# A Nyström attention block with an expert network: the iterated inverse on fewer products, in one stream, with a planner that looks at the end

## The chip, the cores and the metric

The kernel runs on one core of one Trainium2 chip. The metric is device time in microseconds of one execution. A core has five engines that run at the same time and are ordered among each other by semaphores alone: TensorE (PE in the profile; its weight loads are listed as PEld), VectorE (DVE), ScalarE (ACT), GpSimd (POOL) and SyncE (SP, used here only to start DMAs). Each engine works through its own list of instructions in the order in which the program gives them.

## What is computed

The input is 16 sequences of 1024 rows of 256 values, float32 throughout. Cut to what matters:

```
x = x + layernorm(attention(layernorm(x)))
x = x + layernorm(expert_ffn(layernorm(x)))

attention, per sequence and for 16 heads of 16 columns:
    Q, K, V = x @ w_qkv;  Q = Q / 4
    Q_l, K_l = means of 16 successive rows of Q, K        # 64 rows each
    kernel1 = softmax(Q @ K_l.T)                           # 1024 x 64
    kernel2 = softmax(Q_l @ K_l.T)                         # 64 x 64
    kernel3 = softmax(Q_l @ K.T)                           # 64 x 1024
    SV = (kernel1 @ iterative_inv(kernel2)) @ (kernel3 @ V)
    return SV @ w_proj

iterative_inv(K):                                          # 6 iterations
    V = K.T / max(column sums of K)
    for _ in range(6):
        KV = K @ V
        V = (0.25 * V) @ (13 I - KV @ (15 I - KV @ (7 I - KV)))
    return V

expert_ffn: a base product, and for each of 8 experts a hidden layer and a
    reconstruction of the input; the sequence takes the adapter of the expert
    with the smallest reconstruction error
```

The change is about `iterative_inv`, about the order in which the pieces are given to the engines, and about what is prepared before the first batch.

## The kernel before

A batch is one sequence. Its work is cut into stages, each written as a Python generator that yields at the start of every small stretch:

- `stage_a`: turns the normalized rows (`turned_rows`, tile pt_a), makes Q, K and V (pq, pv), the landmark means (`lm`, `bd`), the weights of kernel3 and their product with V (`u`). Its last part normalizes the next batch's input (`norm_a`, tile xa).
- `stage_p`: kernel2 and its inverse V, then w_bd = V times u.
- `stage_c`: kernel1, its product with w_bd, the projection with wproj_sb (po), the normalization and the residual (`added`, tile x1).
- `stage_d1` and `stage_d2`: the norm (`norm`, tile xn_d), the experts' hidden layers (ph) and reconstructions (pr, with the squares of df on ScalarE), the choice of the expert, the gather of its adapter, and the output (pf, y_d).

**The order** of everything on PE, ACT, DVE and POOL is written out before the program is built, by a planner in the same file (`planned`, from line 1192). Each yield carries a name, the names that it follows, and planned times on each engine: `mm(us, tiling, count)` for TensorE and `ew(engine, us, behind, mark)` for the others; a mark "aside" says that nothing that follows waits for that part, "free" that it frees a bank of PSUM. `streams()` makes five lists: stage_a of all batches; stage_p of the even ones; stage_p of the odd ones; stage_c; stage_d1 and stage_d2. At each point the planner tries the next stretch of every stream, runs its model on for AHEAD = 50 us by each of a few rules, and takes the stretch that has lost the least TensorE time by then. `progress` ranks what is ready: a stream of RANK r is meant to be r batches behind stage_a.

Two waits between stages matter. "bd" of batch b in stage_a follows "kp" of batch b - 1 in stage_p, and the products with w_bd in stage_c follow "end" of stage_p. A batch's inverse before the change has 31 stretches: six up to the first V ("kp", "k2", "k2n", "k2t", "rrow", "v0"), four in each of the six iterations ("kv", "sq", "t3", "v"), and "end".

**The inverse** keeps the 16 heads' 64 x 64 matrices as one tile of 128 x 8 x 64: eight on partitions 0 to 63, eight on 64 to 127. `product` (line 552) multiplies all 16 pairs in the 64x64 tiling of TensorE, four independent quarters. Both operands of a matmul lie on the same half of the partitions; which half the result goes to is free. A head is numbered by four bits r, s, t, p2, and `(half, slot)` says which bit chooses the partition half and which bits choose the place. The operand given as lhsT enters transposed, so the kernel keeps V in two forms (`vi` and its transpose `vt`), and K transposed (`k2t`). KV is made twice in an iteration, once with each of two bits as the half (tiles yx and yy, both with 7/3 of the identity taken off), because the third product needs it where the square lies:

```
pkv -> yx = KV - 7/3 I  (halves by x)     yy = KV - 7/3 I  (halves by y)
psq = yx.T yx           sq = psq - 4/3 I
pb  = sq.T yy           t3 = 92/27 I - pb
pvi = vt.T t3  -> vi = 0.25 pvi           pvi = t3.T vt  -> vt = 0.25 pvi
```

Tiles of the inverse come in two sets, `tag{b % 2}`, one for the even batches' stream and one for the odd.

**Before the first batch** the program starts DMAs on ScalarE's queue for all weights, the last of them bd1_rows and bd2_rows; makes the identity and several masks; takes the row means off wproj_sb and wbase_sb (`centre`, lines 148 to 156, on DVE); and transposes the two biases on TensorE (lines 191 to 197). The input of batch 0 is one DMA of 1 MB on SP's queue (`load`, line 116), followed by those of x1.

Of the kernel before, what the change touches and what calls it, by code (L numbers as in the profile page):

```python
# [19 lines left out]
AHEAD, GAP = 50.0, 1.0  # L20
# [25 lines left out]
def kernel(  # L46
# [69 lines left out]
    def load(b, tag, bufs):  # L116
        t = keep.tile([P, NT, D], F32, tag=tag, name=f"{tag}_{b}", bufs=bufs)
        nc.sync.dma_start(out=t, in_=x[b].rearrange("(t p) d -> p t d", p=P))
        live[b][tag] = t
# [13 lines left out]
    bd1_rows = work.tile([E // 2, P], F32, tag="e1", name="bd1_rows")  # L133
    nc.scalar.dma_start(out=bd1_rows, in_=bd1.rearrange("(i r) h -> i (r h)", r=2))
    bd2_rows = work.tile([E * NC, P], F32, tag="e1", name="bd2_rows")
# [18 lines left out]
    for c in range(NC):  # L154
        centre(wproj_sb[:, c, :])
        centre(wbase_sb[:, c, :])
# [34 lines left out]
    bias_ps = one_bank([P, 512], "bias_ps")  # L191
    nc.tensor.transpose(bias_ps[:, 0 : E // 2], bd1_rows, ident[: E // 2, : E // 2])
    nc.tensor.transpose(bias_ps[:, 64 : 64 + E * NC], bd2_rows, ident[: E * NC, : E * NC])
    bd1_sb = const.tile([P, E // 2], F32, name="bd1_sb")
    nc.scalar.copy(bd1_sb, bias_ps[:, 0 : E // 2])
    bd2_sb = const.tile([P, E, NC], F32, name="bd2_sb")
    nc.scalar.copy(bd2_sb.rearrange("p e k -> p (e k)"), bias_ps[:, 64 : 64 + E * NC])
# [36 lines left out]
    def go(name, follows, *parts):  # L234
        return name, follows, parts
# [292 lines left out]
    def stage_p(b):  # L528
# [9 lines left out]
        def mat(tag, name=None):  # L538
            return inv.tile([P, NP, M], F32, tag=f"{tag}{b % 2}", name=f"{name or tag}_{b}")
# [12 lines left out]
        def product(dst, a, c, to, rest):  # L552

            (x, x_at), (y, y_at) = a, c
            frm = x_at[0]
            for g0 in range(2):
                for g1 in range(2):
                    four = [h for h in heads if h[rest[0]] == g0 and h[rest[1]] == g1]
                    for h in sorted(four, key=lambda h: (h[frm] ^ h[to], h[frm])):
                        rows, i = place(*x_at, h)  # L560
                        rows_y, j = place(*y_at, h) if y_at else (rows, None)
                        assert rows_y == rows
                        nc.tensor.matmul(  # L563
                            dst[64 * h[to] : 64 * h[to] + 64, 4 * h[frm] + 2 * g0 + g1, :],
                            lhsT=x[rows, i, :],
                            rhs=y[rows, j, :] if y_at else y[rows, :],
# [13 lines left out]
        kp = inv.tile([P, NC, PC, M], F32, tag=f"yx{b % 2}", name=f"kp_{b}")  # L580
# [12 lines left out]
        mx = small.tile([P, NP], F32, tag=f"mx2{b % 2}", name=f"mx2_{b}", bufs=1)  # L593
# [5 lines left out]
        sm = small.tile([P, NP], F32, tag=f"sm2{b % 2}", name=f"sm2_{b}", bufs=1)  # L599
        nc.vector.tensor_reduce(sm, k2, X, ALU.add)  # L600
        rs = small.tile([P, NP], F32, tag=f"rs2{b % 2}", name=f"rs2_{b}", bufs=1)
# [8 lines left out]
        cs = small.tile([P, NP], F32, tag=f"cs{b % 2}", name=f"cs_{b}", bufs=1)  # L610
# [4 lines left out]
        cmx = small.tile([NP, 2], F32, tag=f"cmx{b % 2}", name=f"cmx_{b}", bufs=1)  # L615
        nc.vector.tensor_reduce(cmx, pcs, X, ALU.max)
        rmx = small.tile([NP, 2], F32, tag=f"rmx{b % 2}", name=f"rmx_{b}", bufs=1)
        nc.vector.reciprocal(rmx, cmx)
        rrow = inv.tile([NP, 2, M], F32, tag=f"yy{b % 2}", name=f"rrow_{b}")
# [4 lines left out]
        rd = small.tile([P, NP], F32, tag=f"rd{b % 2}", name=f"rd_{b}", bufs=1)  # L624
# [4 lines left out]
        x, y = "r", "s"  # L629
        for i in range(N_ITER):  # L630
# [3 lines left out]
            yield step(f"kv{i}", mm(2 * Q, "q64", 128), ew("dve", 0.6, 0), ew("dve", 0.6, 0, "free aside"))  # L634
            pkv = banks_of(f"pkv{i}")
            at_x = product(pkv[0], (k2t, kt_at), (vi, v_at), x, (y, "p2"))
            at_y = product(pkv[1], (k2t, kt_at), (vi, v_at), y, (x, "p2"))
            yx, yy = mat("yx"), mat("yy")
            nc.vector.tensor_tensor(yx, pkv[0], middle(eyes[0], NP), ALU.subtract)
            nc.vector.tensor_tensor(yy, pkv[1], middle(eyes[0], NP), ALU.subtract)  # L640
            parts = [mm(Q, "q64", 64), ew("dve", 0.6, -1, "free")]
            if i == 0:
                parts = [mm(Q, "q64", 64), *parts, ew("act", 0.5, 0, "free aside")]
            yield step(f"sq{i}", *parts)
            if i == 0:
                pvt = banks_of("pvt")
                vt_at = product(pvt[1], (vi, v_at), (eye, None), x, (y, "p2"))
            psq = banks_of(f"psq{i}")
            sq_at = product(psq[0], (yx, at_x), (yx, at_x), y, ("p2", "t"))
            sq = mat("vi", "sq")  # L650
            nc.vector.tensor_tensor(sq, psq[0], middle(eyes[1], NP), ALU.subtract)
            if i == 0:
                vt = mat("vt")
                nc.scalar.copy(vt, pvt[1])
            yield step(f"t3{i}", mm(Q, "q64", 64), ew("dve", 0.6, -1, "free"))
            pb = banks_of(f"pb{i}")
            t3_at = product(pb[0], (sq, sq_at), (yy, at_y), x, ("p2", "t"))
            t3 = mat("yx", "t3")
            nc.vector.tensor_tensor(t3, middle(eyes[2], NP), pb[0], ALU.subtract)  # L659
            more = i < N_ITER - 1  # L660
            yield step(
                f"v{i + 1}",
                mm(*((2 * Q, "q64", 128) if more else (Q, "q64", 64))),
                ew("act", 0.5, 0),
                ew("act", 0.5, 0, "free aside" if more else "free"),
            )
            pv = banks_of(f"pvi{i}")
            if more:
                v_at = product(pv[0], (vt, vt_at), (t3, t3_at), "t", (y, "p2"))
            vt_at = product(pv[1], (t3, t3_at), (vt, vt_at), y, ("t", "p2"))  # L670
            if more:
                vi = mat("vi")
                nc.scalar.mul(vi, pv[0], 0.25)  # L673
            vt = mat("vt")
            nc.scalar.mul(vt, pv[1], 0.25)
            x, y = y, x
# [7 lines left out]
        for r, half in halves():  # L684
            nc.scalar.copy(
                w_bds[b % 2][half, :, r, 0:HD], pw[half, r, 0 : NP * HD].rearrange("x (q d) -> x q d", d=HD)
            )


    def stage_c(b):  # L690
        w_bd = w_bds[b % 2]
        first = [("a", b, "bd"), *([("d", b - 2, "end")] if b >= 2 else [])]
        svt = [None] * NW
# [565 lines left out]
```

## Time and profile before

| | |
|---|---|
| median of three executions | 2420.9 us (2420.38 to 2425.7) |
| the profiled execution | 2422.45 us, span 2420.7 us |
| mean granted TensorE clock | 0.978 |
| DVE: yx, yy, sq, t3 of the inverse | 65.8, 65.3, 65.6, 65.2 us busy, 96 each |
| ACT: vt, vi of the inverse | 56.8 (96) and 47.5 us (80) busy |
| TensorE, products of the inverse by tile | pkv 115.1, psq 66.7, pb 65.5, pvi 65.3 and 57.0, pkt 12.1, pvt 10.9 us busy |

In the profile a group's line has the program line, the engine, the operation, the tile written and the tiles read, the shapes and the count; then busy time in us and the mean of one in ns; then how long the engine stood idle just before such instructions, with what ended it. A line of the timeline has the start, the length and the same names; what stands in brackets is the idle time before it and its releaser. A waits line has the total, the number of times and the longest. Matmuls overlap with their successors, so a group's busy time contains tails that run under the next group. A float32 matmul leaves two records. "issue" is time in which the engine waited for nothing that the profile shows.

### The profile page before, as it was taken

Reading aid. Unit: us, or ns where it says so; the run is one execution under the profiler, and the core shown is the slowest. Engines: PE = TensorE matmul, PEld = TensorE weight load, DVE = VectorE, ACT = ScalarE, POOL = GpSimd, SP = SyncE. Lnnn points to the kernel's source line nnn. Section 1 sums busy time; section 2 is a strip of 40 time slices with the busy share of each in tenths; the row PEclk is TensorE's granted clock in tenths of the full one; section 3 lists DMA queues with packets and bytes.
Section 4 is the critical chain, followed back from the end, with each engine's and each line's share of the span. In section 5 each row is a group of like instructions: output and inputs, shape, how many; then the busy total and the mean of one; then the engine's idle time right before and its main releaser. Section 6 shows DMA issues by size and latency. Waiting matters only on the chain.

```text
span 2420.7 us, 94984 instructions
## 1 busy us (share of the span) xinstructions
PE 2220.6 (92%) x43954; PEld 1458.7 (60%) x43954; DVE 1475.8 (61%) x2811; ACT 1241.5 (51%) x2467; POOL 272.2 (11%) x387
## 2 busy tenths in 40 slices
PE   5998999999999999999999999899999999898865
PEld 3666656575565756657565665656666575665442
DVE  4556576575747666576566657557575666655443
ACT  1333464564546556464745545455454555465545
POOL 1000011020110201011020200202011020111021
PEclk9999999999999999999999999999999999999888
DMA  3000001010010100101010010101001000010000
GB/s 109 19 21 3 20 5 55 2 34 25 5 54 3 57 2 5 54 6 54 2 57 2 14 45 3 55 3 32 27 5 55 2 21 21 5 38 26 15 21 20
DMA packets 56628, 60.94 MB, mean 25 GB/s; under 512 B 4964, under 2 KB 55208, under 8 KB 56232
## 3 DMA queue, kind: packets, MB, share of 16 engines
q1 hardware_dynamic: 50208, 50.35, 6.5%
q8 instruction: 345, 5.65, 0.9%
q0 software_dynamic: 2560, 2.14, 0.3%
q10 hardware_dynamic: 3464, 2.37, 0.3%
q14 instruction: 51, 0.42, 0.1%
HBM read 38.08 MB, written 16.78 MB: 23 GB/s over the span
## 4 chain that ended last, share of the span: by engine, by line
PE 43%; DVE 8%; ACT 7%; issue 2%; POOL 1%; DMA 0%; POOLq 0%; DVEq 0%; ACTq 0%
PE ph L899 5%; PE pq L339 5%; PE pr L932 4%; ACT df L943 3%; PE pf L1033 3%; PE po L829 2%; PE pv L360 2%; PE pvi L563 2%; PE pf L1034 2%; PE pkv L563 2%; PE psv L781 2%; PE psct L752 2%; DVE df L940 2%; DVE mx L417 1%; PE psct L760 1%
## 5 line engine op out<-in xcount | busy, mean ns | idle before, releaser
L943 ACT ACTIVATE df<-df,bd_sb 128x512 f32<-128x512 f32 x512 | 363.3, 711 | 165.4 <-DVE df L940 165.4
L940 DVE TENSOR_TENSOR df<-pr,xt_d 128x1024 f32<-128x1024 f32 x256 | 301.7, 1216 | 107.9 <-PE pr L932 68.5
L932 PE MATMUL pr<-ht,wd_sb 64*64 64x512 f32 x2048 | 251.0, 597 | 3.6 <-ACT ht L907 1.5
L899 PE MATMUL ph<-xt_d,wd_sb 128*128 128x512 f32 x512 | 236.3, 604 | 1.4 <-DVE maxima L722 0.8
L339 PE MATMUL pq<-xt_a,wqkv_sb 128*128 128x512 f32 x512 | 228.1, 600 | 0.0
L722 DVE TENSOR_REDUCE maxima<-psc 128x16 f32<-128x1024 f32 x128 | 150.3, 1217 | 76.9 <-PE psc L714 76.9
L770 ACT ACTIVATE e<-psct 128x1024 f32<-128x1024 f32 x128 | 124.0, 1020 | 115.3 <-PE psct L760 115.2
L417 DVE TENSOR_REDUCE mx<-psm 128x2 f32<-128x1024 f32 x128 | 149.7, 1216 | 33.5 <-PE psm L408 33.5
L339 PEld LDWEIGHTS pq<-xt_a,wqkv_sb 128*128 128x128 f32 x512 | 96.0, 192 | 114.3 <-issue 110.0
L899 PEld LDWEIGHTS ph<-xt_d,wd_sb 128*128 128x128 f32 x512 | 93.1, 191 | 117.1 <-issue 94.6
L453 ACT ACTIVATE e<-psc 128x1024 f32<-128x1024 f32 x128 | 122.8, 1025 | 73.2 <-PE psc L443 71.8
L1033 PE MATMUL pf<-wbase_sb,xt_d 128*128 128x256 f32 x512 | 136.6, 390 | 0.9 <-DVE t L659 0.9
L563 PEld LDWEIGHTS pkv<-vi,k2t 64*64 64x64 f32 x6144 | 104.1, 137 | 44.1 <-issue 18.2
L283 DVE SCALAR_TENSOR_TENSOR y_d<-y_d,rstd_d_y,x 128x256 f32<-128x256 f32 x128 | 53.3, 479 | 124.2 <-POOL rstd_d_y L250 124.1
L248 POOL TENSOR_SCALAR ve_c_y<-ss_c 128x4 f32<-128x4 f32 x32 | 6.2, 195 | 1086.6 <-ACT square_c L294 1086.6
L563 PE MATMUL pkv<-vi,k2t 64*64 64x64 f32 x6144 | 115.1, 223 | 8.0 <-ACT vi L673 3.3
L932 PEld LDWEIGHTS pr<-ht,wd_sb 64*64 64x64 f32 x2048 | 64.9, 133 | 95.5 <-issue 60.6
L829 PE MATMUL po<-wproj_sb,svt 128*128 128x256 f32 x512 | 120.1, 388 | 1.0 <-ACT svt L804 0.9
L781 PE MATMUL psv<-w_bd,e 128*32 128x34 f32 x8192 | 90.3, 198 | 33.0 <-issue 23.5
L781 PEld LDWEIGHTS psv<-w_bd,e 128*32 128x32 f32 x8192 | 80.0, 109 | 61.7 <-issue 35.7
L360 PE MATMUL pv<-wqkv_sb,xt_a 128*128 128x256 f32 x512 | 116.7, 381 | 0.0
L360 PEld LDWEIGHTS pv<-wqkv_sb,xt_a 128*128 128x128 f32 x512 | 95.9, 190 | 22.5 <-issue 7.8
(174 smaller groups left out, 4042.8 us busy)
## 6 DMA issues: line engine op xcount, KB each, us to landing
xa<-in_L_attn_x_dram SPq DMA_DIRECT2D x16, 1024.0 KB
x<-in_L_attn_x_dram SPq DMA_DIRECT2D x16, 1024.0 KB
out_dram<-y_d SPq DMA_DIRECT2D x32, 512.0 KB
wqkv_sb<-in_L_attn_w_qkv_dram ACTq DMA_DIRECT2D x1, 768.0 KB
wd_sb<-in_L_ffn_Wd_dram ACTq DMA_DIRECT2D x2, 256.0 KB
wd_sb<-in_L_ffn_Wd_dram ACTq DMA_DIRECT2D x1, 512.0 KB
wdn<-in_L_ffn_Wa_down_dram,row POOLq DMA_INDIRECT x32, 2.7
wproj_sb<-in_L_attn_w_proj_dram ACTq DMA_DIRECT2D x1, 256.0 KB
```

The source lines that it names most:

```text
L339: nc.tensor.matmul(pq[:, n, :], lhsT=wqkv_sb[:, k, f0 : f0 + P], rhs=xt[:, k, n * 512 : (n + 1) * 512], start=(k == 0), stop=(k == NC - 1),)
L360: nc.tensor.matmul(pv[:, j, :], lhsT=xt[:, k, (t0 + j) * P : (t0 + j + 1) * P], rhs=wqkv_sb[:, k, 2 * D : 3 * D], start=(k == 0), stop=(k ...
L417: nc.vector.tensor_reduce(mx3[:, n, q : q + 2], psc[g], X, ALU.max)
L563: nc.tensor.matmul(dst[64 * h[to] : 64 * h[to] + 64, 4 * h[frm] + 2 * g0 + g1, :], lhsT=x[rows, i, :], rhs=y[rows, j, :] if y_at else y[ro ...
L722: nc.vector.tensor_reduce(mx[:, t0 : t0 + 2, 64 * g : 64 * g + 64].rearrange("x t (p j) -> x p t j", p=2)[:, :, :, 0 : 2 * NC], psc[g].rea ...
L781: nc.tensor.matmul(psv[rows32(g), j // 2, col : col + 2 * (HD + 1)], lhsT=es[p // 2][:, p % 2, j * P + 32 * g : j * P + 32 * g + 32], rhs= ...
L829: nc.tensor.matmul(po[:, j, :], lhsT=svt[n][:, c, j * P : (j + 1) * P], rhs=wproj_sb[:, c, :], start=(c == 0), stop=(c == NC - 1),)
L899: nc.tensor.matmul(ph[:, n, :], lhsT=wd1_sb[:, k, 2 * i : 2 * i + 2, :].rearrange("p e h -> p (e h)"), rhs=xt[:, k, n * 512 : (n + 1) * 51 ...
L932: nc.tensor.matmul(pr[to, r, :], lhsT=wd2_sb[half, i, k * P + 64 * f : k * P + 64 * f + 64], rhs=ht[half, cols], start=True, stop=True,)
L940: nc.vector.tensor_tensor(df, pr, middle(xt[:, k, cols], 2), ALU.subtract)
L943: nc.scalar.activation(df[:, r, :], df[:, r, :], AF.Square, bias=bd2_sb[:, e, k : k + 1], accum_out=part[:, e, k * NW + n : k * NW + n + 1],)
L1033: nc.tensor.matmul(po[:, j, :], lhsT=xt[:, k, cols], rhs=wbase_sb[:, k, :], start=(k == 0), stop=False)
```

## The change

Five parts.

1. **The inverse.** Iterations go in pairs. In the first of a pair KV is made once, by its own product (`x_at`, half h); ScalarE copies it as it is to `xh`. The second form that the third product needs is no longer a product: `across` copies half of y to the other half of the partitions with two ScalarE copies (tile yc), and `product` takes its right operand from y or from that copy, by head. At the end of the first iteration, in place of the new V, the kernel makes the next KV from the old one: `px` = xh.T t3, which is 4 times K times the new V; y of the second iteration is 0.25 px less 7/3 of the identity, again with `across`. V is then made in its transposed form alone (`vt`). At the end of the second iteration both forms of V are made as before. A batch has 28 stretches and 28 products of 16 matmuls, where it had 31 and 37.
2. **One stream of inverses** over all batches instead of two, and one set of its tiles.
3. **Preparations as stretches:** the centring of wproj_sb becomes the first stretch of stage_c, that of wbase_sb with the transposes of the biases the first of stage_d1. bd1_rows and bd2_rows get their buffers from the tag "df".
4. **The load of batch 0's input** in two DMAs, four row blocks each.
5. **The planner:** it looks 70 us ahead instead of 50; progress is the stream's planned TensorE time done, scaled to the number of batches; when less than LAST = 250 us of planned TensorE work is left, each trial runs to the end of the program, counts the end of all engines, and has four more rules that favour the earlier stages.

```diff
-AHEAD, GAP = 50.0, 1.0
+AHEAD, LAST, GAP = 70.0, 250.0, 1.0
...
-        nc.sync.dma_start(out=t, in_=x[b].rearrange("(t p) d -> p t d", p=P))
+        rows = x[b].rearrange("(t p) d -> p t d", p=P)
+        for h in range(2 if b == 0 else 1):
+            part = slice(0, NT) if b else slice(4 * h, 4 * h + 4)
+            nc.sync.dma_start(out=t[:, part, :], in_=rows[:, part, :])
...
-    bd1_rows = work.tile([E // 2, P], F32, tag="e1", name="bd1_rows")
+    bd1_rows = work.tile([E // 2, P], F32, tag="df", name="bd1_rows", bufs=3)
...
-    for c in range(NC):
-        centre(wproj_sb[:, c, :])
-        centre(wbase_sb[:, c, :])
...
+    def prepare_c():
+        yield go(("c", 0, "weights"), [("a", 0, "qk", 0, 0)], ew("dve", 1.9, None))
+        for c in range(NC):
+            centre(wproj_sb[:, c, :])
+
+    def prepare_d():
+        yield go(
+            ("d", 0, "weights"), [("a", 0, "qk", 1, 0)], mm(0.2, "full", 4), ew("act", 0.3, -1, "free"), ew("dve", 1.9, None)
+        )
+        bias_ps = one_bank([P, 512], "bias_ps")
+        nc.tensor.transpose(bias_ps[:, 0 : E // 2], bd1_rows, ident[: E // 2, : E // 2])
+        nc.tensor.transpose(bias_ps[:, 64 : 64 + E * NC], bd2_rows, ident[: E * NC, : E * NC])
+        nc.scalar.copy(bd1_sb, bias_ps[:, 0 : E // 2])
+        nc.scalar.copy(bd2_sb.rearrange("p e k -> p (e k)"), bias_ps[:, 64 : 64 + E * NC])
+        for c in range(NC):
+            centre(wbase_sb[:, c, :])
...
         def mat(tag, name=None):
-            return inv.tile([P, NP, M], F32, tag=f"{tag}{b % 2}", name=f"{name or tag}_{b}")
+            return inv.tile([P, NP, M], F32, tag=tag, name=f"{name or tag}_{b}")
...
+                        yt = y[h[y_at[0]] ^ h[y[2]]] if isinstance(y, tuple) else y
...
+        f, h, g = "t", "r", "s"
+
+        def taken_y(px, scale):
+            y = mat("yx")
+            if scale == 1.0:
+                nc.vector.tensor_tensor(y, px, middle(eyes[0], NP), ALU.subtract)
+            else:
+                nc.vector.scalar_tensor_tensor(y, px, scale, middle(eyes[0], NP), ALU.mult, ALU.subtract)
+            return y
+
+        def across(y):
+            other = mat("yc", "across")
+            frm, to = (t.rearrange("x (f k p) m -> x f k (p m)", f=2, k=2) for t in (y, other))
+            for r, half in halves():
+                nc.scalar.copy(to[64 - 64 * r : 128 - 64 * r, :, r, :], frm[half, :, 1 - r, :])
+            return y, other
+
+        ACROSS = ew("act", 0.33, -1, "aside"), ew("act", 0.33, -1, "aside")
         for i in range(N_ITER):
...
+            if i % 2 == 0:
+                n = 2 if i == 0 else 1
...
+                px, pvt = banks_of(f"pkv{i}")
+                x_at = product(px, (k2t, kt_at), (vi, v_at), h, (g, "p2"))
+                if i == 0:
+                    vt_at = product(pvt, (vi, v_at), (eye, None), h, (g, "p2"))
+                y = taken_y(px, 1.0)
+                xh = mat("xx")
+                nc.scalar.copy(xh, px)
+                if i == 0:
+                    vt = mat("vt")
+                    nc.scalar.copy(vt, pvt)
+                y = across(y)
...
+            sq_at = product(psq[0], (y[0], x_at), (y[0], x_at), g, ("p2", f))
...
+            t3_at = product(pb[0], (sq, sq_at), ((*y, h), (g, (f, h, "p2"))), h, ("p2", f))
+            t3 = mat("vi", "t3")
...
+            if i % 2 == 0:
+                yield step(f"x{i + 1}", mm(2 * Q, "q64", 128), ew("dve", 0.65, 0), ew("act", 0.5, 0, "free aside"), *ACROSS)
+                px, pv = banks_of(f"px{i}")
+                x_at = product(px, (xh, x_at), (t3, t3_at), g, (f, "p2"))
+                vt_at = product(pv, (t3, t3_at), (vt, vt_at), g, (f, "p2"))
+                f, h, g = h, g, f
+                y = taken_y(px, 0.25)
+                vt = mat("vt")
+                nc.scalar.mul(vt, pv, 0.25)
+                y = across(y)
...
     def stage_c(b):
+        if b == 0:
+            yield from prepare_c()
...
     def stage_d1(b):
+        if b == 0:
+            yield from prepare_d()
+
...
-    RANKS = 0, 1, 1, 2, 3
+    RANKS = 0, 1, 2, 3
...
+        return [chain(stages) for stages in ([stage_a], [stage_p], [stage_c], [stage_d1, stage_d2])]
...
+        progress.append([rank + NB * at / sums[-1] for at in sums])
+
+    TOTAL = sum(sums[-1] for sums in before) - 1e-6
...
+            work = self.done()
+            return (self.clock["pe"] if work < TOTAL else max(self.clock.values())) - work + self.gaps
...
+    RULES = [(0.0, 0.1, 0.0), (1.0, 0.1, 0.0), (0.0, 0.3, 0.0), (1.0, 0.3, 0.0)]
+    LAST_RULES = [*RULES, (0.0, 0.1, 0.6), (0.0, 0.1, 1.5), (1.0, 0.1, 0.6), (1.0, 0.1, 1.5)]
...
+            return (wait if wait > 0.15 else 0.0), at - (stay if change == 0.0 else 0.0) + spread * RANKS[k]
...
+            ending = model.done() > TOTAL - LAST
+            limit = TOTAL * 2 if ending else model.clock["pe"] + AHEAD
...
-                    while trial.clock["pe"] <= model.clock["pe"] + AHEAD and (then := trial.next()):
+                    while trial.clock["pe"] <= limit and (then := trial.next()):
```

## The prediction

> **What bounds the kernel.** I read the busy shares first, then five windows of the span, then the groups of TensorE, the waits, and the timeline around the inverse's products.
>
> ```profile
> PE 2220.6 (92%) x43954; PEld 1458.7 (60%) x43954; DVE 1475.8 (61%) x2811; ACT 1241.5 (51%) x2467; POOL 272.2 (11%) x387
> ```
> ```profile
> 0.00:23.00 23.00, 0.76 (x4) 0.66 (x5) 9.17 (x46) 1.52 (x3) 6.63 (x23) 1.00 0.79 240
> 23.00:240.00 217.00, 197.60 (x4147) 136.38 (x4149) 126.06 (x239) 71.71 (x98) 9.19 (x15) 0.95 0.05 17
> 240.00:2180.00 1940.00, 1842.00 (x37517) 1215.68 (x37505) 1231.36 (x2321) 1043.62 (x2073) 220.41 (x303) 0.99 0.08 24
> 2180.00:2335.00 155.00, 131.56 (x2080) 81.89 (x2076) 75.17 (x140) 85.13 (x196) 23.11 (x30) 0.91 0.06 17
> 2335.00:2421.00 86.00, 48.71 (x234) 24.05 (x234) 34.01 (x69) 39.55 (x99) 12.85 (x17) 0.82 0.08 26
> ```
>
> The columns after the length are busy time of PE, PEld, DVE, ACT, POOL, then clock. In the middle 1940 us PE is idle for 98 (5%) while DVE and ACT have a third or more to spare: the middle is bound by TensorE's work. The other 102 idle us are the first 23 (22 idle), the filling (19), the draining (23) and the last batch alone (37).
>
> ```profile
> L563 PE MATMUL pkv<-vi,k2t 64*64 64x64 f32 x6144 | 115.1, 223 | 8.0 <-ACT vi L673 3.3 <-issue 2.4 <-ACT e L770 0.5
> L563 PE MATMUL pb<-yy,sq 64*64 64x64 f32 x3072 | 65.5, 223 | 10.5 <-DVE sq L651 9.9 <-DVE mx L417 0.4
> ```
> ```profile
> 2228.70 1.16 PE L563 MATMUL pkv<-vi,k2t 64*64 64x64 f32 x64
> 2230.77 0.69 PE L563 MATMUL psq<-yx 64*64 64x64 f32 x32 [0.91 <-DVE yx L639]
> 2232.36 0.69 PE L563 MATMUL pb<-yy,sq 64*64 64x64 f32 x32 [0.90 <-DVE sq L651]
> 2233.95 0.69 PE L563 MATMUL pvi<-vt,t 64*64 64x64 f32 x32 [0.89 <-DVE t L659]
> ```
>
> One product of an inverse is 32 records (16 matmuls, two each). The second fence shows an inverse with nothing beside it: 1.59 us from product to product.
>
> **The products removed.** Per batch, before: pkt 1, pvt 1, kv 12, sq 6, t3 6, v 11: 37. After: pkt 1, pvt 1, kv 3, sq 6, t3 6, x and its V 6, v 5: 28. So 9 x 16 = 144 fall away. Price: in the timeline of PE, 87 stretches of exactly one product between other tilings last 0.687 us on average from their start to the next group's start, 35 of two products 1.174. One more product therefore costs 0.487, and entering and leaving the tiling 0.20. 144 x 0.487 = **-70**. Bounds: by undisturbed stretches (1.09 less 0.62) 0.47, -68; by busy time (392.6 us of all seven product groups over 592 products) 0.663, -95, which counts pipeline tails that overlap the next group; so I stay near the first.
>
> **Visits to the tiling.** The 416 64x64 steps before (26 a batch) are joined into 340 visits, since two batches' inverses are in flight and meet. After there are 23 x 16 = 368, each waiting for the one before, so none join: 28 x 0.20 = **+6**; between 0 (joined with the 64x64 pr) and +15 (all 76 joins dear).
>
> **What ACT and DVE gain and lose.** DVE loses yy: 96 x 0.680 = 65 us. ACT loses 48 vi (0.593), gains 48 copies xh (0.58, as L654) and 192 half copies across partitions. The trace has none such; the nearest are the 128x256 copy ut at 0.376 and the 64x512 a_t, which changes partitions, at 0.682 for twice the columns. I take 0.40: 77 us, ACT at some 1318 of 2344, 56%. The scaled y (a scalar_tensor_tensor of 128x512) is priced like the others at 0.68. The halved buffers add no wait of their own, since the next inverse starts behind this one's end anyway. None of the rest is on TensorE as long as it is in time: t3 starts at the earliest two steps after kv, 3.18 us; y is ready at 0.69 + 0.2 + 0.68 = 1.57, the two copies at 2.6. Slack 0.6 if ACT is free; behind a pair of squares (2 x (0.711 + 0.187) = 1.8) they are 1.2 late. The plan doesn't make t3 wait for them, so it may place t3 too soon, and all of PE's later list stands behind it; on ACT the copies wait for y with exps and squares behind them. I take a tenth of 96 places late by 0.5: **+5**, between 0 and 96 x 0.4 = +38.
>
> **The start.**
>
> ```profile
> PE bias_ps L192 <- DMA bd_rows<-in_L_ffn_bd_dram: 19.9, 1, 19.9
> DVE mean L150 <- DMA wbase_sb<-in_L_ffn_W_base_dram: 4.4, 1, 4.4
> ```
>
> Two in-order queues stand behind late DMAs: PE until 19.9, DVE until 19.65, though batch 0's input had landed at 9.3. By 15.3 DVE had all but one of the statistics and had spent 0.85 on centring. Without the centring the last ends near 15.0, the norm begins there instead of at 22.14: **-7**. Bounds: -2.5 (only the centring behind the wait goes) to -9.5 (the first half of the split load also lands, say, a quarter sooner than 9.3, so that half the statistics lie before it). SP issues one DMA more, 0.43 us, ahead of the x1 loads, first read at 240: nothing. The centring (2 x 1.77 us of DVE), two transposes (0.5 of PE) and two tiny ACT copies come back later, in a filling where DVE is busy 126 of 217 us; uncovered they would cost 4.
>
> **The end.** Batch 15's second add_normalized ends at 2322.9, but DVE's list has batch 14's output first, held until 2334.3 by its rstd, so the statistics for 15 start at 2341. From there to the end 80 us are one batch's chain, which no order shortens. A plan that sees the end can have batch 14 done sooner: at most the 23 idle us before 2335 and some 3 of the next. Half: **-12**, between 0 and -26. The same longer look in the middle I put at 0: 5% idle is all there is.
>
> Sum: -70 + 6 + 5 - 7 - 12 = -78. The profiled execution took 2422.45 us (span 2420.7), 1.5 above the median 2420.9: 2344 by it, **2343** as a median.
>
> **Rivals.**
> *More than that* (0.13): all terms at their gains, -95 - 9.5 - 26 = -130: **2292**. For it: with one inverse in flight at a time latency falls from 147 us (batch 0, k2 at 50 to end at 197) or about 230 (later ones), so filling and draining shorten. Against: the middle was 95% full, busy counts tails. The Trainium skill (TensorE: Matmul & The Clock Gate, "Wait — 56ns, not 53.3ns?") says matmuls never start closer than about 25 ns; 32 a product would make 0.8 us and 144 of them -115, an estimate, a total near 2299. The rows disagree: 0.487 us for 32 is 15 ns, in a tiling of four independent tiles.
>
> *The copies are late* (0.10): +38 instead of +5, and nothing gained at the end: 2422 - 70 + 6 - 7 + 38 = **2389**. For it: ACT already waits 165.4 us for DVE with its list in order. Against: the slack of 0.6, and other work usually lies between sq and t3.
>
> *Slower, the single chain sets the end* (0.09): all sixteen inverses now stand in one row, 28 steps each (31 before). The first can't begin before 44, and after the last 185 us followed. A time of 2421 is reached when one inverse takes (2421 - 44 - 185)/16 = 137 us, 4.9 us a step: that is the point from which it decides, and batch 0's pace before was 147 us for 30 steps, also 4.9. At 5.1 it is 143 an inverse, **2517**. Against: undisturbed steps take 1.59, and the plan gives TensorE to the stream that lags. A stage also waits for it sooner: "bd" of batch b needs kp of b-1, now behind the end of b-2.
>
> *Slower, by the clock* (0.02): fewer streams leave holes, and the granted clock in the middle falls from 0.99 to 0.93, near the 0.95 of the filling, when few streams were ready: 0.06 x 1842 = 110 more, **2454**. Half clock comes in stretches of 3.4 us or multiples. The Trainium skill (same page, "HAM oscillation — how this bites in real kernels") warns of TensorE gaps over about 3.4 us; here the longest wait of an inverse's product is under 2.5, which is why I give it little.
>
> *It does nothing* (0.02): TensorE's freed time returns as waiting: 2422. Against it is the 95%.
>
> **How the numbers follow.** The forecast (0.64) covers 2320 to 2368. Faster by over 0.2% (5 us, about what three runs can tell from no change) takes it and the first two rivals: 0.87; same 0.02; slower 0.11. The range runs from the first rival's inner half to past the second: 2300 to 2400; left out are the slower cases, no change and the far ends.
>
> **What would show it.** Product records falling from 592 to 448 products (pkv to 2048 records, pvt now among them); TensorE busy near 2140; first pq near 19 instead of 26; middle idle still about 5%; no wait of pb for ACT over a few us; the last statistics less than 10 us after the last residual add. I am wrong if pb waits for the half copies, if the inverses run back to back with c waiting for w_bd, or if TensorE's idle in the middle grows past 170 us.

## The result, and the profile after

| | before | after |
|---|---|---|
| median | 2423.3 us (2420.38 to 2432.8, 4 runs) | 2361.23 us (2356.43 to 2365.14, 4 runs) |
| ratio | | 0.9738, 95% interval 0.9718 to 0.9757 |
| profiled execution | 2422.45 us, span 2420.7 | 2365.14 us, span 2363.4 |

62 us less, 2.6%. The forecast was 78 less. The kernel before took 2423 to 2426 us in some of the sets of runs and 2490 to 2501 in the others; so ratios to the kernel before of the same set are compared, and 0.1% of them is 2.4 us.

The busy shares of the kernel after:

```profile
PE 2164.1 (92%) x39346; PEld 1387.4 (59%) x39346; DVE 1424.0 (60%) x2715; ACT 1317.5 (56%) x2659; POOL 277.2 (12%) x387
```

TensorE does 56.5 us less and is idle as long as before, 199 us against 200. The same five windows of the kernel after; the middle ends 60 us earlier, the last two have nearly the lengths of before (columns as before):

```profile
0.00:23.00 23.00, 8.38 (x27) 5.67 (x28) 8.74 (x39) 4.06 (x4) 7.00 (x23) 1.00 0.95 282
23.00:240.00 217.00, 201.37 (x3917) 135.51 (x3916) 132.78 (x264) 90.28 (x134) 12.82 (x20) 0.98 0.06 17
240.00:2120.00 1880.00, 1769.55 (x33042) 1137.81 (x33041) 1171.20 (x2202) 1091.60 (x2212) 221.46 (x297) 0.99 0.08 24
2120.00:2275.00 155.00, 133.93 (x2128) 82.78 (x2127) 76.59 (x142) 91.77 (x212) 22.75 (x30) 0.91 0.06 17
2275.00:2363.00 88.00, 50.88 (x238) 25.59 (x236) 34.67 (x70) 39.76 (x99) 13.18 (x18) 0.79 0.08 26
```

The first window has 8 us more of TensorE's work, since the first pq starts 8 us sooner; its line of before, then of after:

```profile
26.07 14.46 PE L339 MATMUL pq<-xt_a,wqkv_sb 128*128 128x512 f32 x32
```
```profile
18.09 14.42 PE L351 MATMUL pq<-xt_a,wqkv_sb 128*128 128x512 f32 x32
```

In the middle it is idle for 110 of 1880 us (5.9%; before 98 of 1940). The end has gained nothing: 88 us with 37 idle, before 86 with 37.

TensorE's groups that answer to the two shown of before, and one that the change doesn't touch, whose line of before stands below it:

```profile
L577 PE MATMUL pkv<-vi,k2t 64*64 64x64 f32 x1536 | 35.2, 229 | 5.3 <-issue 2.6 <-ACT vi L723 1.8 <-DVE vi L641 0.6
L577 PE MATMUL pb<-yx,sq 64*64 64x64 f32 x1536 | 65.3, 223 | 16.3 <-DVE sq L692 8.8 <-ACT e L822 6.3 <-ACT vt L707 0.6
L577 PE MATMUL pb<-across,sq 64*64 64x64 f32 x1536 | 65.0, 223 | 2.1 <-ACT across L662 1.3 <-issue 0.9
L420 PE MATMUL psm<-kt,bd 32*128 32x512 f32 x512 | 93.7, 655 | 5.0 <-ACT e L822 1.2 <-DVE mx L429 0.9 <-DVE svn L844 0.9
```
```profile
L408 PE MATMUL psm<-kt,bd 32*128 32x512 f32 x512 | 86.0, 633 | 1.4 <-DVE k L596 0.5 <-ACT e L770 0.4 <-DVE df L940 0.4
```

The product of K with V is a quarter of what it was, and 592 products of the inverse are 448. The half copies (`across`) made TensorE wait twice, for 1.3 us. But psm, whose 512 matmuls are the same as before, has gone from 86.0 to 93.7 us.

ScalarE's groups that are new in the inverse:

```profile
L662 ACT COPY across<-yx 64x256 f32<-64x256 f32 x192 | 77.4, 403 | 3.4
L707 ACT ACTIVATE vt<-px 128x512 f32<-128x512 f32 x48 | 28.5, 593 | 62.4 <-DVE yx L655 62.1
L683 ACT COPY xx<-pkv 128x512 f32<-128x512 f32 x48 | 28.1, 585 | 67.2 <-DVE yx L653 67.1
```

The copies across cost what was forecast, 0.40 us. The other two rows hold something else: 129 us in which ScalarE stood idle until VectorE's y was done, which reads the same PSUM tile. In some 88 of them its own product had been done. The engines take turns on the tile, as one step near the end shows, in the timeline of TensorE, then VectorE, then ScalarE:

```profile
2153.89 0.69 PE L577 MATMUL pkv<-vi,k2t 64*64 64x64 f32 x32 [0.86 <-ACT vi L723]
...
2154.72 0.69 DVE L653 TENSOR_TENSOR yx<-pkv,eye 128x512 f32<-128x512 f32 x1 [3.08 <-PE pkv L577]
...
2155.45 0.59 ACT L683 COPY xx<-pkv 128x512 f32<-128x512 f32 x1 [1.12 <-DVE yx L653]
2156.05 0.82 ACT L662 COPY across<-yx 64x256 f32<-64x256 f32 x2
```

`xx` begins 0.04 us after y ends, though its product had been done since 2154.6. The copies across end 2.98 us after the product's start; the prediction had 2.6, since it let them follow y directly.

Another view of TensorE serves for what follows. **Occupancy** of a group: from the start of each of its stretches in TensorE's timeline to the start of the next group's, summed; it takes in waits and the changing of the tiling, and the groups together make the span. A **tiling change** is a place where two successive groups differ in tile shape.

| | before | after |
|---|---|---|
| occupancy of the inverse (kv, sq, t3, x, v, pkt, pw) | 395.0 us | 330.2 us |
| psm, pr, psc, put, pt_d together | 666.6 us | 700.3 us |
| psv and psct together | 253.2 us | 234.7 us |
| tiling changes | 1121 | 1185 |

### The profile page after: what moved, and what is told of

It is laid out like the page before. It is cut to its first block, busy times and chain, and to the rows that moved or that the text cites. A ratio compares the mean times of both kernels' runs of the same rounds, so it can differ in the third digit from the quotient of the medians.

```text
span 2363.4 us, 85848 instructions
## 1 busy us (share of the span) xinstructions
PE 2164.1 (92%) x39346; PEld 1387.4 (59%) x39346; DVE 1424.0 (60%) x2715; ACT 1317.5 (56%) x2659; POOL 277.2 (12%) x387
## 4 chain that ended last, share of the span: by engine, by line
PE 42%; DVE 8%; ACT 7%; issue 3%; POOL 1%; DMA 0%; POOLq 0%; DVEq 0%; ACTq 0%
PE ph L954 6%; PE pq L351 5%; PE pr L987 4%; PE pf L1088 3%; ACT df L998 3%; PE po L881 3%; DVE df L995 2%; PE pf L1089 2%; PE pv L372 2%; PE psct L804 2%; PE psv L833 2%; PE put L483 1%; PE psct L812 1%; DVE mx L429 1%; PE psm L420 1%
## 5 line engine op out<-in xcount | busy, mean ns | idle before, releaser
L692 DVE TENSOR_TENSOR sq<-psq,eye 128x512 f32<-128x512 f32 x96 | 65.8, 686 | 96.8 <-PE psq L577 93.8
L698 DVE TENSOR_TENSOR t<-eye,pb 128x512 f32<-128x512 f32 x96 | 65.3, 680 | 90.7 <-PE pb L577 90.4
L962 ACT ACTIVATE ht<-ph,bd_sb 128x1024 f32<-128x1024 f32 x64 | 71.0, 1109 | 74.6 <-PE ph L954 74.3
L881 PEld LDWEIGHTS po<-wproj_sb,svt 128*128 128x128 f32 x512 | 96.4, 192 | 25.5 <-ACT svt L856 4.4
L1088 PEld LDWEIGHTS pf<-wbase_sb,xt_d 128*128 128x128 f32 x512 | 96.9, 193 | 18.9 <-issue 4.0
```

Source lines behind the costliest of these rows:

```text
L881: nc.tensor.matmul(po[:, j, :], lhsT=svt[n][:, c, j * P : (j + 1) * P], rhs=wproj_sb[:, c, :], start=(c == 0), stop=(c == NC - 1),)
L1088: nc.tensor.matmul(po[:, j, :], lhsT=xt[:, k, cols], rhs=wbase_sb[:, k, :], start=(k == 0), stop=False)
```

## The experiments

**The plan of ScalarE's copies.** The plan lets `xx` and `vt` start beside y; the trace shows them behind it. First edit: tell the plan so.

```diff
-                    ew("act", 0.5, 0, "aside" if i == 0 else "free aside"),
+                    ew("act", 0.5, 1, "aside" if i == 0 else "free aside"),
...
-                yield step(f"x{i + 1}", mm(2 * Q, "q64", 128), ew("dve", 0.65, 0), ew("act", 0.5, 0, "free aside"), *ACROSS)
+                yield step(f"x{i + 1}", mm(2 * Q, "q64", 128), ew("dve", 0.65, 0), ew("act", 0.5, 1, "free aside"), *ACROSS)
```

> Changed kernel, with one thing told to the planner: ScalarE's copy out of a PSUM tile that VectorE reads too (xx and vt) begins behind VectorE's y, not beside it; the instructions are the same, only their order may differ. Theory A (the missing gain of some 16 us lies in ScalarE's list, which stands still behind y 64 times for 129 us that the plan doesn't count, so that TensorE waits for banks that ScalarE frees late): TensorE's waits for ACT in the middle fall from about 38 to under 25 us, time 2340 to 2352. Theory B (the missing gain is the price of one stream of inverses, fewer stretches to choose from): 2355 to 2365, no change. Theory C (orders scatter by themselves): any change within 8 us either way, without a matching change in the waits for ACT.

Measured: 2386.95 us, 0.9846 (0.9826 to 0.9866), 1.1% slower than after. TensorE's waits for ScalarE did fall, from 47 to 31 us over the span, and ScalarE's own waits for y too:

```profile
L707 ACT ACTIVATE vt<-px 128x512 f32<-128x512 f32 x48 | 28.4, 593 | 50.2 <-DVE yx L655 50.2
L683 ACT COPY xx<-pkv 128x512 f32<-128x512 f32 x48 | 27.8, 580 | 40.8 <-DVE yx L653 40.8
```

Yet waits for "issue" rose from 39 to 55 us, and the occupancy of psv from 98 to 115. What the truer plan won at the copies, its order lost elsewhere.

Second edit: beside that, the copies across are issued in the stretch of the square, and the third product waits for them in the plan.

```diff
-        ACROSS = ew("act", 0.33, -1, "aside"), ew("act", 0.33, -1, "aside")
+        ACROSS = ew("act", 0.4, None, "aside"), ew("act", 0.4, None)
...
-                y = across(y)
-            yield step(f"sq{i}", mm(Q, "q64", 64), ew("dve", 0.6, -1, "free"))
+            yield step(f"sq{i}", mm(Q, "q64", 64), ew("dve", 0.6, -1, "free"), *ACROSS)
...
+            y = across(y)
```

> As e1, and the two half copies of y are given to ScalarE one stretch later, with the square, when y has long been written; the plan lets t3 wait for them. Theory A: waits for ACT fall further, ScalarE's own idle time before xx and vt remains (it is the bank that makes them wait) but none before the copies, time 2335 to 2350. Theory B: 2355 to 2365. The rival that t3 itself is late for want of the copies: the waits of pb (14 us in the middle) fall by half and the time by 5 to 8.

Measured: 2402.65, 0.9908 (0.9892 to 0.9924), slower still. The third product now starts within 0.35 us of the copies' end in 14 of 96 places instead of 5, as they come later. But TensorE's waits for ScalarE are 42 us, less than the 47 of after, while psc has 242 us of occupancy for 228 and po 126.5 for 118. So the lateness of copies is not what this run loses most by. Both edits leave TensorE's instructions as they were: another order of them can cost 26 and 41 us.

**One stream, alone.** The kernel before, with its old inverse, planner and preparations, but one list of inverses:

```diff
-    RANKS = 0, 1, 1, 2, 3
+    RANKS = 0, 1, 2, 3
...
-            chain([stage_p], range(0, NB, 2)),
-            chain([stage_p], range(1, NB, 2)),
+            chain([stage_p]),
```

> Kernel before with one stream of inverses, all else as before (its tiles stay two sets, its own planner). Theory B: slower than before by 10 to 25, 2431 to 2446. Theory A: within 6 of before, 2415 to 2427. The single chain as the bound, a rival of the prediction (31 stretches at 4.9 us and more): 2440 or above with c waiting for w_bd.

Measured: 2462.07, 1.0145 (1.0121 to 1.0169): **+35 us**. Tiling changes rise from 1121 to 1195. The inverse itself takes 11 us more of occupancy; pr 12, psc 12, psm 5 and put 5 more. The step is within what another order alone can cost, so how much of it belongs to one stream is open.

**The new inverse, alone, in one stream.** The planner of before (50 us, no end), the preparations of before and one load:

```diff
-AHEAD, LAST, GAP = 70.0, 250.0, 1.0
+AHEAD, GAP = 50.0, 1.0
...
-        for h in range(2 if b == 0 else 1):
...
+    for c in range(NC):
+        centre(wproj_sb[:, c, :])
+        centre(wbase_sb[:, c, :])
...
-    def prepare_c():
...
-    def prepare_d():
```

> Kernel before with the new inverse in one stream and nothing else of the change: its own planner, its own preparations, one load. e4 gave the single stream without the new inverse, ratio 1.0145 to before. If the 144 products are worth what the prediction says (70 us, 2.9%), the ratio is 0.985 (0.980 to 0.990) and the rest of the change (start 8 us, planner) accounts for 1.1% up to 0.9738. If a product is worth its busy time (0.663, 95 us), 0.975. If the single stream's price vanishes with the shorter inverse, 0.970 to 0.976, and the planner is worth nothing beyond the start.

Measured: 2463.07 beside 2490.43, 0.9888 (0.9871 to 0.9905). Against the old inverse in one stream that is 1.0145 - 0.9888 = 2.6%, **-62 us**. From here to the kernel after are another 1.5%, 36 us, for the start, the planner and the end.

**The price of a product.** Each square is made twice, the first time into the other half of its PSUM tile; the plan counts it.

```diff
-            yield step(f"sq{i}", mm(Q, "q64", 64), ew("dve", 0.6, -1, "free"))
+            yield step(f"sq{i}", mm(2 * Q, "q64", 128), ew("dve", 0.6, -1, "free"))
...
-            sq_at = product(psq[0], (y[0], x_at), (y[0], x_at), g, ("p2", f))
+            for dst in psq[::-1]:
+                sq_at = product(dst, (y[0], x_at), (y[0], x_at), g, ("p2", f))
```

> Changed kernel that makes every square of an inverse twice, the second time into the unused half of the same PSUM banks, and tells the plan so: 96 products more and nothing else. It measures what one product is worth. At 0.487 us each (prediction): 47 us, ratio to before 0.993 (from 0.9738). At 0.663 (busy time): 64 us, 1.000. At 0.8 (32 starts of 25 ns): 77 us, 1.005. If TensorE's work doesn't set the time: below 0.985.

Measured: 2476.6, 0.9943 (0.9922 to 0.9964). The ratio is 0.0205 above that of after. In this set, where the kernel before takes 2490, that makes 51 us for 96 products, **0.53 us** each (0.43 to 0.64 with the far ends of both intervals). The start-to-start price 0.487 is inside; the busy price 0.663 and the 0.8 of the 25 ns rule are not. But the order has changed too, and the first edit to the plan shows that this alone can cost 26 us. The trace settles it without the order: in 88 stretches of two products or more of the inverse, the 33rd record starts 0.521 us after the first on average, and 0.523 in 91 such stretches of the kernel before.

**The planner.** Three settings of one line. No look at the end:

```diff
-AHEAD, LAST, GAP = 70.0, 250.0, 1.0
+AHEAD, LAST, GAP = 70.0, -1.0, 1.0
```

> Changed kernel whose planner never looks at the end (LAST below zero, so the four extra rules and the runs to the end are never used). If the look at the end is worth what the prediction put on it, 12 us, the time rises to 2373 and the stretch from batch 15's last residual to its statistics grows beyond the 19 us it has now. If it is worth nothing, since batch 14's output stands ahead of batch 15's statistics in one stream whatever the rules, 2356 to 2366 and the same 19 us.

Measured: 2436.92 beside 2500.95, 0.9744 (0.9723 to 0.9765): the look at the end is worth nothing that can be told. The gap from the last residual to its statistics is 19.5 us in this trace (2336.3 to 2355.8).

A look of 71 us, to see how much hangs on the order that happens to come out:

```diff
-AHEAD, LAST, GAP = 70.0, 250.0, 1.0
+AHEAD, LAST, GAP = 71.0, 250.0, 1.0
```

> Changed kernel with AHEAD 71 instead of 70: nothing but another order out of the same planner. It measures how far an order scatters by itself. Theory C, after e1 and e2 (2387 and 2403 with a plan that counts ScalarE's wait): orders scatter by 10 to 25, so 2350 to 2385 anywhere. If orders hardly scatter, 2358 to 2366, and the 25 and 41 us of e1 and e2 have a cause of their own.

Measured: 2441.42, 0.9765 (0.9742 to 0.9789), 0.3% over after, in a widely different order.

The old look of 50 us:

```diff
-AHEAD, LAST, GAP = 70.0, 250.0, 1.0
+AHEAD, LAST, GAP = 50.0, 250.0, 1.0
```

> Changed kernel with AHEAD 50 as before the change. Between c1 (the new inverse alone, 0.9888) and the changed kernel (0.9738) lie 1.5%, of which the start is 8 us, 0.3%; for one stream the new progress is nearly the old one, and the look at the end was worth nothing in e5. If the longer look of 70 us is the rest: 0.982 to 0.988. If it isn't, 0.971 to 0.977 as e9's 71, and the rest is what an order brings by chance.

Measured: 2413.28 beside 2425.53, 0.9944 (0.9925 to 0.9963), **2.1% or 50 us** over after. The middle window of this run, and the wait that grew most:

```profile
240.00:2175.00 1935.00, 1803.43 (x32760) 1149.58 (x32759) 1175.93 (x2199) 1095.20 (x2218) 214.99 (x295) 0.98 0.08 24
```
```profile
PE psv L833 <- issue: 21.6, 18, 1.9
```

132 us idle in the middle, and over the span TensorE is busy for 29 us more than after (2193.0 for 2164.1) with the same instructions; occupancy of the inverse 358 instead of 330, of psc 246 instead of 228, of psct 148 instead of 137. Waits of psv for "issue" are 21.6 us here and 11.9 after.

**Two streams again.** The changed planner on the kernel before, with its two streams:

```diff
-AHEAD, GAP = 50.0, 1.0
+AHEAD, LAST, GAP = 70.0, 250.0, 1.0
...
-            stream_progress.append(rank + b + (at[b] - us) / max(of_batch[b], 1.0))
...
+        progress.append([rank + NB * at / sums[-1] for at in sums])
```

> Kernel before with the changed planner (AHEAD 70, progress by the stream's whole work, the look at the end), two streams and the old inverse. Prediction's reading (the planner's part is worth only the end, 0 to 12): 2410 to 2424. If the planner makes up for the single stream's price in the change, it must be worth 15 to 30 here: 2395 to 2410.

Measured: 2515.23, 1.0056 (1.0037 to 1.0074). And the kernel after with two streams and two sets of tiles; both sets fit into the memory only if df has two buffers instead of three:

```diff
-            return inv.tile([P, NP, M], F32, tag=tag, name=f"{name or tag}_{b}")
+            return inv.tile([P, NP, M], F32, tag=f"{tag}{b % 2}", name=f"{name or tag}_{b}")
...
-                    df = buf4k("df", [P, 2, 512], f"df_{b}_{i}_{k}_{n}", 3)
+                    df = buf4k("df", [P, 2, 512], f"df_{b}_{i}_{k}_{n}", 2)
...
-    RANKS = 0, 1, 2, 3
+    RANKS = 0, 1, 1, 2, 3
```

> Changed kernel with two streams of inverses and two sets of their tiles, and to make room for them two buffers of df instead of three. From e4, where one stream in place of two cost the kernel before some 36 us: if that price holds here too, 2325 to 2340, with about 60 fewer changes of tiling than 1185. If the new planner or the shorter inverse has taken that price away, 2350 to 2370. The buffer of df may cost up to 10 where ScalarE's squares run behind.

Measured: 2504.14, 1.0009 (0.9996 to 1.0023), 2.8% slower than after, with only 1078 tiling changes. Neither tells what two streams are worth here: the new measure of progress gives both streams the same start, though the odd one is a batch later, and df has lost a buffer. How the new inverse would do in two streams with the old measure of progress was not tried.

**The end.** The profile after shows what holds it, in VectorE's timeline:

```profile
2261.57 1.67 DVE L295 SCALAR_TENSOR_TENSOR x<-y_c,rstd_c_y,x 128x256 f32<-128x256 f32 x4 [3.73 <-POOL rstd_c_y L262]
2275.36 1.67 DVE L295 SCALAR_TENSOR_TENSOR y_d<-y_d,rstd_d_y,x 128x256 f32<-128x256 f32 x4 [12.12 <-POOL rstd_d_y L262]
2280.47 1.67 DVE L295 SCALAR_TENSOR_TENSOR y_d<-y_d,rstd_d_y,x 128x256 f32<-128x256 f32 x4 [3.44 <-POOL rstd_d_y L262]
2282.05 0.42 DVE L254 BATCH_NORM_STATS2 st_d<-x 128x6 f32<-128x256 f32 x1
```

Batch 15's x is ready at 2263.2; its statistics start at 2282.05, behind batch 14's output. That is 18.8 us, before 18.1, as these two lines of before show:

```profile
2321.25 1.65 DVE L283 SCALAR_TENSOR_TENSOR x<-y_c,rstd_c_y,x 128x256 f32<-128x256 f32 x4
...
2341.01 0.42 DVE L242 BATCH_NORM_STATS2 st_d<-x 128x6 f32<-128x256 f32 x1
```

In `streams()` stage_d1 of batch 15 follows stage_d2 of batch 14 in one list, so no rule of the planner can turn them round. First try: the norm of stage_d1 moves to the end of stage_c, with a tile of its own.

```diff
+            xns[h] = work.tile([P, 4, D], F32, tag="xn", name=f"xn_d{b}_{h}")
...
+        turned = [("d", b - 1, "xt", h) for h in range(NW)] if b >= 1 else []
+        yield from norm(b, "d", src, [[("c", b, "out", h), *turned] for h in range(NW)], dst, "d")
+
+    def stage_d1(b):
```

> Changed kernel with the norm ahead of the experts (statistics and normalized rows xn_d) moved from the head of stage_d1 to the end of stage_c, in tiles of their own, so that batch 15's no longer stand behind batch 14's output in one stream. If that order is why the look at the end gained nothing: the gap from the last residual to the last statistics falls from 19 us to under 3, batch 15's transposes begin 8 to 12 us after the last residual instead of 24, and the ratio falls from 0.9738 to 0.967 to 0.971. If the end is bound by something else (TensorE's work of batch 14, the buffer of xt_d): the gap shrinks and the time stays at 0.972 to 0.976.

Measured: 2457.6 beside 2490.43, 0.9864 (0.9843 to 0.9885), 1.3% slower than after. The same wait of TensorE in the kernel after and in this one (total, times, longest, in us):

```profile
PE pf L1089 <- POOL a_t L1066: 9.8, 6, 3.8
```
```profile
PE pf L1091 <- POOL a_t L1068: 50.5, 7, 9.9
```

The output product pf needs a_t, three of whose rows GpSimd fills with two memsets; in its list these now stood behind the norm's rstd, in 7 of 16 batches directly. Second try: the memsets come directly behind the gathers, and each half's statistics directly behind its residual.

```diff
+            yield go(("d", b, "stats", h), [("c", b, "out", h)], *STATS)
+            stats_d.append(stats_of(live[b]["x1"][:, 4 * h : 4 * h + 4, :], f"d{b}_{h}", "d"))
...
+        a_t = work.tile([R + 3, N], F32, tag="ht", name=f"a_t_{b}")
+        nc.gpsimd.memset(a_t[R : R + 3, :], 1.0)
+        nc.gpsimd.memset(a_t[R : R + 2, :], 0.5)
         yield go(("d", b, "wup"), [("d", b, "gather")], ew("dve", 0.8, None))
```

> h1 mended: the two memsets of a_t are given to GpSimd right behind the adapter's gathers instead of behind the next batch's rstd, and the statistics of each half follow that half's residual. In h1 TensorE waited 50 us for those memsets (about 1 in the changed kernel), 2.0% of its time. If that wait is what undid h1, the ratio falls from 0.9864 to 0.964 to 0.972 and the end is 8 us shorter than in the changed kernel. If the norm in stage_c disturbs the order by itself, 0.974 to 0.985 with the wait gone.

Measured: 2408.98 beside 2491.13, **0.9676** (0.9655 to 0.9697): better than after, 0.9738 (0.9718 to 0.9757), by 0.6% or 15 us, and the best of all versions. TensorE's waits for GpSimd are 1.0 us in all; in the kernel after they are 9.8, as shown, not the 1 that the expectation names. An order alone can move more than 0.6%, so the ratio by itself doesn't show that the end gained it; the timeline does. VectorE's timeline at the last residual:

```profile
2322.16 1.67 DVE L295 SCALAR_TENSOR_TENSOR x<-y_c,rstd_c_y,x 128x256 f32<-128x256 f32 x4 [3.89 <-POOL rstd_c_y L262]
2323.75 0.42 DVE L254 BATCH_NORM_STATS2 st_d<-x 128x6 f32<-128x256 f32 x1
```

The statistics follow at once. From the start of the last residual to the end of the span are 85 us (2407.2 - 2322.2), after 102 (2363.4 - 2261.6).

## Why the prediction was right, and where it was not

The total came out at -62 for -78 forecast, inside the likeliest case. That is partly luck: two terms that were mis-sized have opposite signs.

| step | predicted | what the runs show |
|---|---|---|
| 144 products removed | -70 | -75 (144 x 0.52) |
| visits to the tiling, one stream | +6 | +35 (one stream alone) |
| copies and across | +5 | not separated: 1.3 us of direct waits, some 21 more for ScalarE |
| start | -7 | -8.0 |
| end | -12 | 0 |
| longer look in the middle | 0 | -28 to -50 |

The right column doesn't add up to -62, since its terms come from different runs and each run has an order of its own. The runs that lead step by step from before to after do: one stream +35, the new inverse in it -62, the rest -36 (start 8, so some 28 for the planner), together -63. In that chain the new inverse with its copies is worth some 13 us less than its products alone; where these went was not separated.

**Products: right.** The price from start to next start held, 0.487 forecast and 0.52 in the traces; the busy price and the 25 ns rule did not. The Trainium skill's 25 ns (TensorE: Matmul & The Clock Gate, "Wait — 56ns, not 53.3ns?") would be 0.8 us for 32, an estimate; the traces disagree: 0.52 us for 32 is 16 ns a record, in this tiling of four independent quarters. Product records fell to 448 products, as said.

**Visits: the step that failed by size.** "Visits to the tiling" counted the 28 more visits that the inverse would make, and 20 more came (360 for 340). But where two batches' products no longer meet, the order of everything else changes too. Tiling changes rose by 74 with one stream alone and by 64 after. The forecast's 0.20 us is for entering and leaving, two changes, so they account for 6 to 7 us. Most of the cost lay outside the inverse (28 of 39 us of span in the run with one stream alone), as in psm's 655 ns for 633 above. That the rest is order is the likeliest reading and is not shown. TensorE's busy time fell to 2164 and not to 2140, since groups that the change leaves alone became busier, psm by 7.7 us and psc by 4.7.

**The longer look: the other failed size.** "The same longer look in the middle I put at 0: 5% idle is all there is" is wrong twice: the idle share doesn't bound the gain, since a better order makes busy time and occupancy smaller as well (29 us of busy time between 50 and 70), and in one stream idle time is larger without it. The value is not sharp: 28 us by one pair of runs, which holds the measure of progress too, 50 by the other, and 70 against 71 differ by 0.3%. How much of it is the rule and how much the one order that came out stays open.

**The end: failed as a mechanism.** "A plan that sees the end can have batch 14 done sooner" overlooked that both sit in one list. The gap between the last residual and its statistics, forecast under 10 us, stayed at 18.8, and leaving out the look at the end changed nothing. Moving the norm out of that list removed the gap; with the memsets moved too it gave 0.6%, 15 us, and the end alone is 17 us shorter in the timeline.

**Copies: right in cost, wrong in path.** 0.40 us each and ScalarE at 1317 us were forecast. That y holds up `xx` and `vt` was not, so in the step shown above the slack to the third product is 3.18 - 2.98 = 0.2 instead of 0.6. The Trainium skill has the rule (PSUM — Partial Sum Buffer, "PSUM bank collisions raise a hardware error"): two engines may not touch one bank's same part at once, two readers included, and the compiler puts them in order. The trace agrees: ScalarE's copy began behind VectorE's read in 64 waits of 129 us in all. It cost little here, since other work usually lies between the square and the third product: TensorE's waits for ScalarE rose from 25 to 47 us, and the two runs that planned for it had fewer such waits and were slower. Why a truer plan gave worse orders was not settled.

**Start: right.** The first pq begins at 18.09 instead of 26.07. VectorE's statistics begin at 7.47, when the first half has landed (before at 9.29), and VectorE no longer stands behind wbase_sb.

**The rivals.** The inverses do run in one row: k2 of batch 0 at 40.8 and of batch 15 at 2087.1 are 136.4 us apart per batch, at the 137 from which the rival counted. At that pace the rival's own sum gives 44 + 16 x 136.4 + 185 = 2411, 50 us over the time measured. No stage was seen waiting for w_bd, and a step takes 4.9 us where 1.6 would do: the row looks as slow as the plan lets it be, and not like what sets the end. The clock stayed at 0.99 in the middle.

## What to carry to other kernels

Price an operation on a full engine from its start to the next one's start, and count what a change of order does to the neighbours' mode changes as well as its own. A low idle share doesn't say that a better order can't win: order also changes how long the same instructions take. Where a stage waits at the end, look first whether a list written in the program holds it; and when its work moves, look at every queue it passes, GpSimd's too. When one program takes two times, compare the two traces record by record: the difference can lie in a few short stretches.

## What was not expected of the hardware

The same kernel took 3% longer in some of the sets of runs. The kernel after and the one without the look at the end give TensorE its work in nearly the same order, and fall into two such sets. The same wait in the first and in the second:

```profile
PE psv L833 <- issue: 11.9, 9, 2.2
```
```profile
PE psv L833 <- issue: 20.5, 28, 1.8
```

All of TensorE's waits for "issue" are 39 us in the first and 72 in the second. The long matmuls hardly differ (occupancy of pq 226.2 and 225.7, pv 114.8 and 114.8, ph 234.7 and 233.0); the short ones do: psv 97.9 and 112.2, put 86.6 and 101.0, the inverse 330.2 and 348.3, psc 227.7 and 237.5.

The Trainium skill (Runtime: NRT & Kernel Launch, "Instruction fetch mechanics") has the fetching of instructions hidden behind a sequencer that dispatches more slowly. The trace of the kernel after shows that part of it is not hidden. TensorE's instructions come in 309 packets of 16 KB (q8 in the page) for some 79,000 instructions, 256 each. Of its 34 waits for "issue", 33 stand at the same place of these 256, and each of these ends 1.2 to 1.7 us after such a packet landed, so 37.9 of 38.6 us go to fetching. The second run has 33 such waits too, 32 us.

The other 39 us of the second run are something else. They are 68 waits, and 66 of them fall within 1 us of the stretches of some 5 us in which the packets of GpSimd's gathers of the adapter move (q0), once a batch. The gather of the fifth batch in the kernel after, then in the run without the look at the end (columns as in the windows above):

```profile
916.00:921.10 5.10, 5.10 (x182) 4.00 (x178) 1.84 (x4) 5.03 (x12) 4.03 (x6) 1.00 0.12 29
```
```profile
926.60:931.70 5.10, 2.03 (x22) 1.40 (x22) 0.04 (x1) 0.70 (x4) 4.03 (x6) 0.74 0.10 26
```

Over all sixteen gathers TensorE starts 20.6 records a us in the first and 6.0 in the second. Compared record by record, 70 of the 72 us by which the second span is longer arise in these sixteen stretches, 148 us long. Every trace of a set with the longer times has it (5.5 to 8.7 records a us), none of a set with the shorter ones (17.1 to 24.4). By the record the longer sets ran on chips 4, 7 and 11 and the shorter ones on 1 and 6, where one is named. Why a gather holds the engines up on some chips and not on others is not shown.

This bears on the ratios. If a long set adds the same time to both kernels, its ratios lie 0.1 to 0.2% too near 1. The run without the look at the end, in nearly the order of after, gave 0.9744 in a long set for 0.9738 in a short one.
